# Transposing the attention weights in two halves of 64 rows, two heads at a time

## The chip, the cores and the metric

The kernel runs on one NeuronCore of a Trainium2 chip. The core has a matrix engine (TensorE, PE in the profile; its weight loads are listed apart as PEld), a vector engine (VectorE, DVE), a scalar engine (ScalarE, ACT), a general engine (GpSimd, POOL) and a synchronisation engine (SyncE, SP) that issues most DMAs. Matrix results land in PSUM, which has eight banks of 512 float32 columns on 128 partitions; everything else lives in SBUF. The metric is the device time of one execution in microseconds, lower is better.

## The reference

The program is a stack of two layers on a tensor `x` of 16 sequences of 512 tokens with 256 channels, all in float32. Four sub-layers follow each other, each with a residual and a layer norm:

1. latent attention with 16 heads: queries, keys and values are widened to 32 latent channels per head, rotated by position, and `softmax(q k^T)` is causal over 512 tokens;
2. a gated feed-forward layer whose inputs and weights are rounded to blocks of 4-bit floats;
3. a recurrence over the 512 tokens, with 16 heads of 64 states;
4. a token-mixing feed-forward layer.

The part that matters here is the attention:

```
att = einsum('bhql,bhkl->bhqk', q_for_k, k_lat) * L ** (-0.5)
att = where(causal, att, -inf); att = softmax(att, axis=-1)
y_lat = einsum('bhqk,bhkl->bhql', att, v_lat)
```

The weights `att` come out with the query token on the partitions. The second product sums over the key token, so the key token has to be on the partitions, and every 128 by 128 block of the weights is transposed in between.

## The kernel before, in words

The kernel has two long stages. The first, up to about 1757 us, does sub-layers 1 and 2, and the change is in it. The second, from about 1800 us, does sub-layers 3 and 4.

The first stage runs over 16 sequences `b`, four groups `g` of four heads, and three slots `n` (lines 799 to 834). The 512 queries are four blocks `i` of 128, and block `i` needs keys `0..i`, which is `i+1` blocks of 128 by 128. `BLOCKS` (line 521) puts block 3 in slot 0 (four key blocks), block 2 in slot 1 (three) and blocks 1 and 0 in slot 2 (two and one, three together). So each slot has four heads, and each head has three or four blocks to transpose: ten blocks per head and group, 2560 in all.

A slot goes like this.

- `scores` (line 526) issues the `S` products of its four heads into four PSUM banks. They contract over 32 latent channels, so each head uses 32 rows of the array and the four heads use different rows (line 534). VectorE then adds the mask, takes the row minimum (the scores are negated) and writes `p` to SBUF (line 546).
- `exponentials` (line 554) makes `p = exp(...)` with its row sum on ScalarE, two heads behind.
- `turn` (line 565) transposes the `p` of one head of the slot before on TensorE, three or four blocks into one PSUM bank (line 569), and ScalarE copies the bank to SBUF as `pT` (line 571).
- After the third slot of a group, `weighted` (line 576) multiplies all twelve `pT` with the values in 80 matrix instructions, four heads' worth side by side in quarters of 32 output rows (`py`, line 600).

Between these the kernel puts pieces of other work: projections (`heads` L449, `latents` L467 and L486, `values` L431, `out_projection` L501) and the feed-forward layer of an earlier sequence (`ffn_up`, `ffn_down`, which multiply through L164 and transpose at L293 and L333). `Beside.half_slot` (line 693) hands out these pieces in the order of a written plan, at an even pace, twice per head and so eight times per slot. `divide` (line 607) transposes the reciprocals of the row sums (L614) and divides `py`.

TensorE executes its instructions in exactly the order of the program text (`manual_schedule`). The other engines work through queues whose order the tile framework's planner sets when the kernel is built. Each PSUM tile of 512 columns comes from `mm` (line 152), which walks round a ring of seven banks; a tile must be read out before its bank comes round again. An eighth bank holds `py`.

The array works in shapes. Most products use all 128 rows and 128 columns. `S` uses four strips of 32 rows, the `latents` products of L467 use two halves of 64 rows (q in one, k in the other), and `py` uses four strips of 32 columns. A transpose is one matrix instruction with the data as the loaded weights and an identity as the moving operand; an ordinary float32 product takes two matrix instructions.

The pools that the change touches are `ptp`, with 14 buffers of 512 columns for `pT` (line 791), and the ring of banks.

Of the kernel before, what the change touches and what calls it, by code (L numbers as in the profile page):

```python
# [10 lines left out]
F32 = mybir.dt.float32  # L11
# [8 lines left out]
P = 128  # L20
B, T, C = 16, 512, 256
NT = T // P
# [37 lines left out]
def tile_kernel(ctx: ExitStack, tc: tile.TileContext, I: dict, out: bass.AP):  # L60
    nc = tc.nc
# [90 lines left out]
    def mm(name):  # L152
        banks.append(banks.pop(0))
        return banks[-1].tile([P, 512], F32, tag="mm", name=name)
# [198 lines left out]
    with ExitStack() as a:  # L353
# [44 lines left out]
        for i in range(2):  # L398
            nc.gpsimd.tensor_copy(bd["bdqs"][:, i::2], bd["bdq"][:, 1 - i :: 2])
            at = COLS["q2lb"][0]  # L400
# [161 lines left out]
                )  # L562
            return p

        def turn(n, p):
            w = sum(i + 1 for i, _ in BLOCKS[n]) * P
            ps = mm("ps_pt")
            for at in range(0, w, P):
                nc.tensor.transpose(ps[:, at : at + P], p[:, at : at + P], ident)  # L569
            pT = ptp.tile([P, T], F32, tag="pT", name="pT")  # L570
            nc.scalar.copy(pT[:, :w], ps[:, :w])  # L571
            return pT

        undivided = []

        def weighted(b, g, pTs):

            if g % 2 == 0:
                weighted.py = ps_y.tile([P, 2, 2, P], F32, tag="y", name="py")
            py = weighted.py[:, g % 2]  # L580

            rc = small.tile([P, 16], F32, tag="rc", name="rc")
            nc.vector.reciprocal(rc, sum_of.pop((b, g)).rearrange("p c e h -> p (c e h)"))  # L583
            rcx = att.tile([P, 2, P], F32, tag="rcx", name="rcx")
            nc.gpsimd.tensor_copy(  # L585
                rcx.rearrange("p c (n d) -> p (c n) d", d=16),
                rc.unsqueeze(2).to_broadcast([P, 16, 16]),
            )
            quarters = [[], [], [], []]
            for n, blocks in enumerate(BLOCKS):  # L590
                for i, at in blocks:
                    for h in range(4):
                        for j in range(i + 1):
                            pt = pTs[n * 4 + h][:, at + j * P : at + j * P + P]
                            quarters[PLACE[i][0] * 2 + h // 2].append((i, j, h, pt))
            for q in quarters:
                q.sort(key=lambda e: e[:3])
            for four in zip(*quarters):
                for q, (i, j, h, pt) in enumerate(four):
                    nc.tensor.matmul(  # L600
                        py[q * 32 : q * 32 + 32, PLACE[i][1], :], vpad[b % 2][:, j, g * 4 + h, :], pt,
                        start=j == 0 and h % 2 == 0, stop=j == i and h % 2 == 1,
                        skip_group_check=True,
                    )
            undivided.append((b, g, py, rcx))
# [182 lines left out]
                pass  # L788

        pp = a.enter_context(tc.tile_pool(name="pp", bufs=9))  # L790
        ptp = a.enter_context(tc.tile_pool(name="ptp", bufs=14))
        ps_b = five.enter_context(tc.tile_pool(name="ps_b", bufs=5, space=PSUM))
        ps_y = five.enter_context(tc.tile_pool(name="ps_y", bufs=1, space=PSUM))
        banks[:] = [ps_2] * 2 + [ps_b] * 5
# [3 lines left out]
        with tc.manual_schedule(engines={mybir.EngineType.PE}):  # L798
# [4 lines left out]
            for slot in slots + [None]:  # L803
# [14 lines left out]

                for h in range(4):
                    beside.half_slot()  # L820
                    if before:
                        pTs.append(turn(before[0][2], before[1][h]))
                    if slot:
                        behind.append((*slot, h, *tiles[h]))
                        ps.append(tiles[h][0])
                    while len(behind) > (LAG if slot else 0):
                        exponentials(*behind.pop(0))
                    if h == 1:
                        divide()
                    beside.half_slot()  # L830
# [484 lines left out]
```

## Time and profile before

| what | value |
|---|---|
| device time, median of 3 | 2539.11 us (2538.06 to 2540.24) |
| profiled execution, span from first to last instruction | 2543.7 us |
| mean granted TensorE clock | 0.980 |
| PE busy / DVE busy / ACT busy / POOL busy | 95% / 76% / 64% / 41% |
| transposes of `p` (L569) | 2560 matrix instructions, mean 280 ns, 396.3 us busy |
| copies to `pT` (L571) | 768, mean 517 ns, 374.2 us busy |
| products with the values (L600) | 5120 matrix instructions, mean 274 ns |

The profile gives each instruction's start and duration. Matrix instructions are pipelined: the duration of one is its way through the array, and several overlap, so the pace of a sequence is read from the starts of successive rows of the timeline and not from the mean duration. The profiled execution's span is 4.6 us above the median of the timed runs. "Idle before" in a row is the time for which the engine had nothing in flight, with the instruction that ended it.

### The profile page before, as it was taken

The page shows a single profiled execution, that of the slowest core. Times are in us where ns is not written, and L with a number is a line of the kernel's source. Part 1 is how long each engine was busy: PE and PEld are TensorE (multiplying, and loading weights), DVE is VectorE, ACT ScalarE, POOL GpSimd, SP SyncE. Part 2 cuts the span into 40 slices and gives each one's busy share as a digit, 9 for nine tenths or more (in the row PEclk, how much of TensorE's full clock was granted, in tenths as well). Part 3 has the DMA queues.
Part 4 walks back from the last instruction along what each step waited for, and adds up shares of the span by engine and source line. Part 5 has one row for each costly group of instructions (what it writes and reads, how often), then busy time and mean ns, then how long its engine had stood idle before and what let it go on. Part 6 is the DMA issues. An engine that isn't in the chain of part 4 may idle for free.

```text
span 2543.7 us, 73791 instructions
## 1 busy us (share of the span) xinstructions
PE 2412.0 (95%) x28802; PEld 1712.7 (67%) x28802; DVE 1925.8 (76%) x5492; ACT 1621.3 (64%) x5536; POOL 1035.4 (41%) x1642
## 2 busy tenths in 40 slices
PE   7789999999999999999999999998799999999998
PEld 4455666666666666666666666655678888888885
DVE  4867888788888888888888888867756666666666
ACT  4656676676766666666666666654366666666664
POOL 4322333333333333333333333332445555555554
PEclk8889999999999999999999999989899999999999
DMA  3000000000000000000000000000111111111100
GB/s 117 24 9 6 12 24 14 16 16 12 24 14 16 16 12 24 14 16 16 12 24 14 16 14 6 16 14 9 43 32 39 37 40 41 40 38 39 36 28 27
DMA packets 58015, 61.30 MB, mean 24 GB/s; under 512 B 7873, under 2 KB 53058, under 8 KB 57666
## 3 DMA queue, kind: packets, MB, share of 16 engines
q1 hardware_dynamic: 56802, 55.54, 7.0%
q8 instruction: 226, 3.70, 0.6%
q14 instruction: 123, 1.01, 0.1%
q10 hardware_dynamic: 864, 1.05, 0.1%
HBM read 39.79 MB, written 16.78 MB: 22 GB/s over the span
## 4 chain that ended last, share of the span: by engine, by line
PE 51%; DVE 29%; ACT 10%; POOL 5%; issue 3%; DMA 1%; ACTq 0%; DVEq 0%; POOLq 0%; SPq 0%
PE u L1076 8%; DVE p L546 5%; PE ps_pt L569 5%; PE u L1036 5%; ACT p L559 4%; PE S L534 3%; PE ps_d L164 3%; DVE q_q L210 3%; ACT pT L571 3%; PE pg L164 3%; PE pu L164 2%; PE ps_h L449 2%; DVE q_sc L205 2%; DVE q_q L218 2%; PE ps_a L916 2%
## 5 line engine op out<-in xcount | busy, mean ns | idle before, releaser
L559 ACT ACTIVATE p<-p,nm 128x512 f32<-128x512 f32 (+3 forms) x1024 | 570.4, 562 | 492.3 <-DVE nm L546 488.3
L1084 ACT ACTIVATE hist<-u 64x64 f32<-64x64 f32 x2048 | 447.1, 218 | 237.4 <-PE u L1076 151.4
L546 DVE CUSTOM_DVE_ANT_0 p<-S,mask 128x512 f32<-128x512 f32 (+3 forms) x1024 | 442.9, 484 | 50.9 <-PE S L534 50.4
L1076 PEld LDWEIGHTS u<-hist,ta 128*64 128x64 f32 x8176 | 367.7, 138 | 119.9 <-ACT hist L1084 41.5
L569 PEld LDWEIGHTS ps_pt<-ident,p 128*128 128x128 f32 x2560 | 302.0, 142 | 217.3 <-issue 107.1
L571 ACT COPY pT<-ps_pt 128x384 f32<-128x384 f32 (+1 forms) x768 | 374.2, 517 | 62.3 <-PE ps_pt L569 62.1
L569 PE MATMUL ps_pt<-ident,p 128*128 128x128 f32 x2560 | 396.3, 280 | 4.5 <-DVE nm L546 3.0
L1076 PE MATMUL u<-hist,ta 128*64 128x32 f32 x8176 | 394.4, 218 | 4.6 <-ACT hist L1084 4.5
L219 POOL TENSOR_TENSOR q_q<-q_q,q_m 128x704 f32<-128x704 f32 (+1 forms) x140 | 164.1, 1172 | 372.2 <-DVE q_q L218 361.5
L534 PE MATMUL S<-kc,qr 32*128 32x512 f32 (+3 forms) x2048 | 224.1, 475 | 10.5 <-ACT qr L488 7.9
L1036 PE MATMUL u<-xt,wb 128*64 128x64 f32 x4128 | 224.9, 231 | 5.1 <-issue 5.0
L559 ACT ACTIVATION_READ_ACCUMULATOR p<-p,nm 128x1 f32 x1024 | 199.8, 195 | 0.0
L164 PE MATMUL ps_d<-wdT,hT 128*128 128x256 f32 x732 | 173.1, 386 | 13.9 <-DVE nm L546 12.1
L164 PE MATMUL pg<-wgT,xqT 128*128 128x352 f32 x512 | 177.9, 471 | 6.5 <-DVE nm L546 5.1
L483 POOL TENSOR_TENSOR qc<-qc,qs 128x512 f32<-128x512 f32 x64 | 81.5, 1273 | 235.5 <-DVE qs L482 221.1
L164 PE MATMUL pu<-wuT,xqT 128*128 128x352 f32 x512 | 173.7, 462 | 1.0 <-DVE nm L546 1.0
L1036 PEld LDWEIGHTS u<-xt,wb 128*64 128x64 f32 x4128 | 166.7, 140 | 10.3 <-issue 5.5
L600 PEld LDWEIGHTS py<-pT,vpad 128*32 128x32 f32 x5120 | 138.7, 110 | 47.0 <-issue 30.3
L600 PE MATMUL py<-pT,vpad 128*32 128x128 f32 x5120 | 162.6, 274 | 7.8 <-ACT pT L571 7.5
L164 PEld LDWEIGHTS ps_d<-wdT,hT 128*128 128x128 f32 x732 | 135.4, 192 | 37.6 <-DVE nm L546 15.4
L86 POOL TENSOR_SCALAR ve<-mv 128x2 f32<-128x2 f32 (+1 forms) x160 | 31.1, 194 | 312.4 <-DVE mv L94 309.7
L585 POOL COPY rcx<-rc 128x256 f32<-128x256 f32 x64 | 40.3, 630 | 286.9 <-DVE rc L583 260.9
(167 smaller groups left out, 4648.8 us busy)
## 6 DMA issues: line engine op xcount, KB each, us to landing
xT<-in_xT_dram SPq DMA_DIRECT2D x16, 512.0 KB
x<-in_x_dram SPq DMA_DIRECT2D x16, 512.0 KB
xs<-x SPq DMA_DIRECT2D x64, 128.0 KB
x<-xs SPq DMA_DIRECT2D x32, 256.0 KB
xm<-xs SPq DMA_DIRECT2D x32, 256.0 KB
out_dram<-o SPq DMA_DIRECT2D x64, 128.0 KB
w<-in_w_down_dram SPq DMA_DIRECT2D x2, 352.0 KB
w<-in_w_gate_dram SPq DMA_DIRECT2D x5, 128.0 KB
```

Source lines behind the costliest of these rows:

```text
L164: nc.tensor.matmul(dst, left, right, start=start, stop=stop)
L219: last.tensor_tensor(q, q, m, ALU.subtract)
L483: nc.gpsimd.tensor_tensor(of[k], of[k], x, ALU.add)
L534: nc.tensor.matmul(S[h][:, at : at + w], q[rs, i * P : i * P + P], k[rs, :w], start=True, stop=True,)
L546: nc.vector.tensor_tensor_reduce(out=p[:, own], in0=S[h][:, own], in1=mask[:, T - (i + 1) * P :], scale=1.0, scalar=-MASKED, op0=ALU.add, ...
L559: nc.scalar.activation(p[:, own], p[:, own], AF.Exp, bias=nm[:, u : u + 1], scale=-1.0, accum_out=sum_of[b, g][:, cb, half, h : h + 1],)
L569: nc.tensor.transpose(ps[:, at : at + P], p[:, at : at + P], ident)
L571: nc.scalar.copy(pT[:, :w], ps[:, :w])
L600: nc.tensor.matmul(py[q * 32 : q * 32 + 32, PLACE[i][1], :], vpad[b % 2][:, j, g * 4 + h, :], pt, start=j == 0 and h % 2 == 0, stop=j == i ...
L1036: nc.tensor.matmul(u[rs, k, par:n:2, bs : bs + 16], wb[:, g * 2 + k, par, half, rs], xt[:, g, at : at + n - par : 2, :], start=par == 0 an ...
L1076: nc.tensor.matmul(into[cs, :, c, :], ta[:, t % 2, g * 2 + k, cs], own[:, :, c, :], start=False, stop=True, skip_group_check=True,)
L1084: nc.scalar.activation(state[g][rs, :, r * 32 : r * 32 + 32].rearrange("p k (s b) -> p k s b", s=2), u[rs, :, t - t0, :] .rearrange("p k ( ...
```

## The change

`turn` now takes two heads. It asks for two PSUM banks. Every block of `p` is cut into its upper and lower 64 rows (64 query tokens each), and each half is transposed by an instruction of its own with a 64 by 64 piece of the identity: the upper half through rows 0 to 63 of the array into the first bank, the lower half through rows 64 to 127 into the second. A bank thus holds the same half of all blocks of both heads, with 64 columns per block. Two copies on ScalarE, one per bank, put the halves side by side in a `pT` tile of 2 x 512 columns, so that a block is again 128 contiguous columns for `weighted`. The loop calls `turn` at the second and fourth head of a slot for two heads at once. `ptp` has 7 buffers of twice the size.

```diff
-        def turn(n, p):
-            w = sum(i + 1 for i, _ in BLOCKS[n]) * P
-            ps = mm("ps_pt")
-            for at in range(0, w, P):
-                nc.tensor.transpose(ps[:, at : at + P], p[:, at : at + P], ident)
-            pT = ptp.tile([P, T], F32, tag="pT", name="pT")
-            nc.scalar.copy(pT[:, :w], ps[:, :w])
-            return pT
+        def turn(n, two):
+
+            w = sum(i + 1 for i, _ in BLOCKS[n])
+            ps = [mm("ps_pt") for _ in range(2)]
+            halves = [t.rearrange("p (u n t) -> p u n t", u=2, t=64) for t in ps]
+            for u, p in enumerate(two):
+                for at in range(w):
+                    for r in range(2):
+                        rs = slice(r * 64, r * 64 + 64)
+                        nc.tensor.transpose(
+                            halves[r][:, u, at, :], p[rs, at * P : at * P + P], ident[rs, rs],
+                        )
+            pT = ptp.tile([P, 2, NT, 2, 64], F32, tag="pT", name="pT")
+            for r in range(2):
+                nc.scalar.copy(pT[:, :, :w, r, :], halves[r][:, :, :w, :])
+            return pT.rearrange("p u n r t -> p u (n r t)")
...
-                            pt = pTs[n * 4 + h][:, at + j * P : at + j * P + P]
+                            pt = pTs[n * 2 + h // 2][:, h % 2, at + j * P : at + j * P + P]
...
-        ptp = a.enter_context(tc.tile_pool(name="ptp", bufs=14))
+        ptp = a.enter_context(tc.tile_pool(name="ptp", bufs=7))
...
-                    if before:
-                        pTs.append(turn(before[0][2], before[1][h]))
+                    if before and h % 2:
+                        pTs.append(turn(before[0][2], before[1][h - 1 : h + 1]))
```

## The prediction

> **What bounds the kernel now.** I read the page's slices first, then the busy time of the steady stretch, then the chain that ended last over the attention stage, then the groups of the changed lines by shape, and last the PE timeline for the pace of single instructions.
>
> ```profile
> PE   7789999999999999999999999998799999999998
> ...
> 370.00:1525.00 1155.00, 1121.83 (x9183) 762.07 (x9181) 958.13 (x2807) 775.23 (x2313) 414.11 (x480) 1.00 0.05 16
> ```
>
> The second line has PE, PEld, DVE, ACT and POOL busy in 1155 us of the steady stretch: PE 97%, DVE 83%, ACT 67%, at full granted clock. The change lies only in the stage up to 1757 us.
>
> ```profile
> by line: DVE p L546 7.5%; PE ps_pt L569 7.4%; ACT p L559 5.8%; PE S L534 4.9%; PE ps_d L164 4.6%; DVE q_q L210 4.5%; issue 3.8%; ACT pT L571 3.8%; PE pg L164 3.6%; PE pu L164 3.5%; DVE q_q L218 3.4%; DVE q_sc L205 3.4%; PE ps_h L449 3.3%; D
> ```
>
> This is the chain over 45 to 1757 us. PE is almost always occupied, yet the chain runs through VectorE about as often: in each sequence of some 106 us there are stretches of 30 us in which PE work follows PE work, and stretches of 20 and 40 us in which VectorE does and PE is barely ahead. The transposes have 7.4% of 1712 us, 127 us.
>
> ```profile
> L569 PE MATMUL ps_pt<-ident,p 128*128 128x128 f32 x2560 | 396.3, 280 | 4.5 <-DVE nm L546 3.0 <-ACT xqT L295 0.7 <-ACT pT L571 0.4
> ...
> L571 ACT COPY pT<-ps_pt 128x384 f32<-128x384 f32 x512 | 228.9, 482 | 38.8 <-PE ps_pt L569 38.6
> ...
> L571 ACT COPY pT<-ps_pt 128x512 f32<-128x512 f32 x256 | 145.4, 587 | 23.5 <-PE ps_pt L569 23.5
> ```
>
> The pace, and what a change of the array's shape costs, is in the timeline (start, length of the row, engine, line, count):
>
> ```profile
> 104.52 0.20 PEld L235 LDWEIGHTS ps_t<-ident,wq 64*128 64x128 f32 x2 [0.56 <-POOL wq L220]
> 104.53 0.33 PE L235 MATMUL ps_t<-ident,wq 64*128 64x64 f32 x2 [0.32 <-DVE nm L546]
> ...
> 916.66 0.49 PE L569 MATMUL ps_pt<-ident,p 128*128 128x128 f32 x3
> 916.99 1.89 PE L431 MATMUL ps_v<-wv,xT 128*128 128x256 f32 x8
> ...
> 920.28 0.55 PE L569 MATMUL ps_pt<-ident,p 128*128 128x128 f32 x3
> 920.75 0.69 PE L467 MATMUL ps_qs<-heads,bdqs 64*128 64x512 f32 x1
> ...
> 925.64 0.69 PE L467 MATMUL ps_q<-heads,bdq 64*128 64x512 f32 x1
> 925.65 0.69 PE L467 MATMUL ps_k<-heads,bdk 64*128 64x512 f32 x1
> 926.17 0.59 PE L467 MATMUL ps_q<-heads,bdq 64*128 64x512 f32 x1
> 926.18 0.59 PE L467 MATMUL ps_k<-heads,bdk 64*128 64x512 f32 x1
> 926.70 0.66 PE L569 MATMUL ps_pt<-ident,p 128*128 128x128 f32 x4
> ...
> 1398.54 0.49 PE L569 MATMUL ps_pt<-ident,p 128*128 128x128 f32 x3
> 1398.96 0.62 PE L600 MATMUL py<-pT,vpad 128*32 128x128 f32 x10
> 1400.07 2.17 PE L600 MATMUL py<-pT,vpad 128*32 128x128 f32 x70 [0.49 <-ACT pT L571]
> ```
>
> Three transposes followed by work of the same shape take 916.99 - 916.66 = 0.33 us, so 109 ns each. Three between works of other shapes take 920.75 - 920.28 = 0.47 us: 0.14 more, which is the first weight load no longer hidden (row of 0.55 us instead of 0.49, some 55 ns) and about 90 ns to empty the array. Leaving the 64-row shape also takes 90 ns (926.70 - 926.18 = 0.52 us for 512 columns, which take 0.43 us elsewhere), and a plain product then shows its load too (0.69 instead of 0.59 us, 104 ns). The q and k products in the two row halves start 0.01 us apart and both run at full pace.
>
> **The change part by part.**
>
> *Transposes.* Out go 2560 x 109 ns = 279 us of PE pace. In come 5120 half transposes, two per block. The trace has four 64-row transposes, all in one half of the array (L235): the second load starts 0.20 - 0.138 = 0.06 us after the first, and the second matrix instruction (223 ns long, the shortest of that tile) starts 0.33 - 0.223 = 0.11 us after the first, of which 55 ns are the unhidden load. So one half costs 57 ns, with its load hidden beside the one before. If the two halves run beside each other, as the q and k products do, a block costs 57 ns: 2560 x 57 = 146 us. If they don't, it costs 2 x 57 = 114 ns: 292 us. I take 57, since the q and k rows are the nearest case of two row halves with float32 operands and separate banks, and keep 114 for the range. Issuing is no limit: the 70 `py` instructions of the last line above start within 2.17 - 0.27 = 1.9 us, with as many loads, 14 ns per instruction; two halves with their loads are four instructions in 57 ns, the same pace.
>
> A rule of the skill speaks against this. The row says that a 64-row load of 128 columns lets the next one start after 0.06 us. The Trainium skill ("TensorE: Matmul & The Clock Gate", section on LDWEIGHTS) says that a weight load takes its columns divided by 1.2 in nanoseconds, however few rows it has; that would be an estimated 107 ns per half, the load would set the pace, and the sum below would turn from a saving into an estimated 30 us of loss. The trace's plain loads agree with the page (104 ns), its transposes' loads don't (55 ns), and the measured row decides.
>
> *Changes of shape.* I went through PE's instructions between the first and the last transpose of `p` in trace order, and counted places where the shape (128 x 128, 64 or 32 rows, or 32 columns) differs from the instruction before: 626. With each even head's transposes moved to behind those of the odd head, and all of them of 64-row shape, it is 1040. Going in costs 93 ns + 55 ns for the load, coming out 90 ns + 104 ns (55 where another transpose follows): 171 ns on average. 414 x 171 ns = 71 us more. The gain from next to the L467 products, which have the same shape, is in this count.
>
> *PE in sum:* -133 + 71 = -62 us of 1712.
>
> *What of that reaches the end.* 127 of the transposes' 279 us lie on the chain, a share of 0.45. The rest lies where VectorE's queue sets the pace and PE would only wait longer. -62 x 0.45 = -28 us. The ends: nothing of it passes, or all of it (-62).
>
> *Copies.* 768 before and after, of the same 384 or 512 elements per partition; the reads are two runs per bank, the writes runs of 64. A copy of 256 elements in runs of 16 (`vpad`, L437) has a mean of 371 ns and a contiguous one (`rT`, L616) 376, so I count no change in length. They lie beside PE work on an engine that is 67% busy. What changes is when they come: two in a row after every second head. Behind them in ScalarE's queue wait exponentials, the tanh of the gate (L309) and the copies of others; VectorE waits on that tanh for 94 us in all.
>
> *The wait before `py`.* In the third group of each sequence `py` follows the last transposes directly, and already waits 0.49 us for the last copy (1400.07). Now both copies of the last pair must be done before the first product with either head: one more copy, 0.48 us, 16 times, 8 us. In the other three groups 1.1 to 2.4 us of other PE work lie in between, which cover 0.97 us of copies and the way to them, the 1.1 us just so. The 8 us count at the same 0.45: +4 us. Queued behind `py` are the next slot's `S`, on which VectorE's line 546 waits.
>
> *Earlier demands that fall away.* Heads 0 and 2 are transposed about two half slots later, so their exponentials are surely ready; these waits were 3.0 us (row of L569) and I count nothing. Bank use is unchanged in number, two at a time out of the ring of seven, and `pT` has the same bytes.
>
> *Sum:* -28 + 4 = -24 us on the profiled execution's 2543.7, so 2519.7; that execution lies 4.6 us above the median of the runs, so 2515 us.
>
> **The rivals.**
>
> 1. *The halves don't run beside each other.* For it: no row shows two transposes in two row halves. Against it: q and k. Price: 292 - 279 + 71 = +84 us of PE; at 0.45 +38, and as PE then binds nearly everywhere up to all of it: 2577 to 2623 us. The point from which it decides is 81 ns per block: (279 - 71)/2560.
> 2. *VectorE takes over.* It is 83% busy with 17 us of idle time in 106, most of it waits of about 1 us for POOL and ScalarE. If its queue absorbs what PE gains, the time is 2534 to 2544. For it speaks the chain's VectorE share, against it the PE stretches of 30 us per sequence.
> 3. *ScalarE's paired copies delay VectorE.* If each of the 128 tanh of the gate waits one copy (0.48 us) longer and VectorE with it, that is +61 us, or -28 + 61 = +33 at worst; half of it gives 2541, and the range is 2544 to 2572. For it: the chain already goes exponentials, two copies, tanh, VectorE. Against: before, these copies also stood there, only one at a time.
> 4. *All of PE's gain passes*, since PE is 97% busy: 2543.7 - 62 - 4.6 = 2477, to 2495.
>
> **How the numbers follow.** My forecast, a share of about one half passing, 2495 to 2534: 0.49. Rival 1: 0.17. Rival 2: 0.11. Rival 3: 0.12. Rival 4: 0.11. A range of 2480 to 2570 leaves out rival 1 and a little of rivals 3 and 4, 2 in 10; the likeliest case alone is 2495 to 2534. A difference of 0.2% (5 us) is about what a measurement of this kernel can tell from none: faster 0.60, same 0.11, slower 0.29.
>
> **What would show it.** Right: 5120 transposes of shape 64*128 with 64x64 operands, pairs starting about 57 ns apart with the second half a few ns behind the first; stretches of 0.34 us (six pairs) or 0.46 us (eight) plus about 0.34 us of changing; PE's share falls and its waits for VectorE grow; copies still 482 and 587 ns. Wrong: halves that start 57 ns apart in turn, so 114 per block (rival 1); `py` waiting 1 us and more in more than one group; more idle time of VectorE before line 310 (rival 3); a chain with PE's share unchanged and longer transposes. The forecast falls if a change of shape costs more in the new place than between L569 and L467, or if the planner orders VectorE's queue in another way.

## The result, and the profile after

The change makes the kernel slower: 2556.66 us (median of 4, 2553.82 to 2559.43) beside 2539.68 us (2538.06 to 2543.98) for the kernel before. The ratio is 1.0063, with a 95% interval of 1.0049 to 1.0078. The prediction was 2515 us. The time lies inside the range given with it (2480 to 2570), but on the other side of the time before, so the direction was wrong.

The profiled execution of the kernel after has a span of 2557.6 us, 13.9 more than that of before. First the slices of its page: busy tenths of TensorE and VectorE, and the granted clock.

```profile
PE   7778999999999999999999999997799999999998
...
DVE  6756788887878878888787887887756666666666
...
PEclk9789999999999999999999999999899999999999
```

TensorE's start is emptier than before (7, 7, 7, 8 in the first slices, 7, 7, 8, 9 before), and the rest of its row reads almost the same. The steady stretch, with the same columns as before (PE, PEld, DVE, ACT, POOL, clock, DMA):

```profile
370.00:1525.00 1155.00, 1106.04 (x10823) 708.17 (x10822) 943.18 (x2772) 761.20 (x2274) 404.04 (x473) 1.00 0.05 16
```

TensorE is busy for 15.8 us less of the 1155 than before (1121.83), and VectorE and ScalarE also do less in the same time (958.13 and 775.23 before): all three wait more. The chain of work that ended last, over the attention stage (45 to 1771 us):

```profile
by line: DVE p L546 12.0%; PE S L534 5.9%; ACT p L559 5.6%; PE py L608 5.4%; DVE q_q L210 4.6%; issue 4.3%; PE ps_pt L574 4.0%; PE ps_h L449 3.9%; PE pg L164 3.9%; ACT pT L579 3.8%; PE pu L164 3.3%; DVE q_sc L205 3.1%; DVE q_m L214 2.7%; DV
```

The transposes fell from 7.4% to 4.0% of it, as they should. In their place VectorE's line 546, which reads the `S` banks, went from 7.5% to 12.0%, and `py` is in it with 5.4%. The groups of the changed lines (L574 are the half transposes, L579 the copies; busy us in all, mean ns of one, idle time before them):

```profile
L574 PE MATMUL ps_pt<-ident,p 64*128 64x64 f32 x5120 | 251.1, 231 | 12.3 <-DVE nm L546 8.9 <-ACT pT L579 2.1 <-DVE qc L477 0.6
...
L579 ACT COPY pT<-ps_pt 128x384 f32<-128x384 f32 x512 | 218.0, 483 | 58.3 <-PE ps_pt L574 58.1
...
L579 ACT COPY pT<-ps_pt 128x512 f32<-128x512 f32 x256 | 137.1, 593 | 9.9 <-PE ps_pt L574 9.1
```

Four rows of TensorE's timeline in the kernel after (start, length of the row, line, count):

```profile
1250.46 0.59 PE L574 MATMUL ps_pt<-ident,p 64*128 64x64 f32 x12
1250.97 1.14 PE L534 MATMUL S<-kc,qr 32*128 32x512 f32 x8
...
1371.93 0.66 PE L574 MATMUL ps_pt<-ident,p 64*128 64x64 f32 x16
1372.52 0.44 PE L622 MATMUL ps_r<-ident,rcx 128*128 128x128 f32 x2
```

These rows carry the change's own mechanism. Eight pairs that follow work of the same shape take 1372.52 - 1371.93 = 0.59 us with the way out of the shape; six that come after another shape take 1250.97 - 1250.46 = 0.51 us. Starts inside a turn show a new pair every 61 to 64 ns (mean 62.7; the second pair after a change of shape comes 111 ns behind the first, as the load shows) and the second half mostly 3 to 4 ns behind the first. So the halves do run beside each other. The copies keep their 483 and 593 ns (482 and 587 before).

What TensorE waits for in the steady stretch of the kernel before (line that waits, what released it, us in total, times, longest):

```profile
PE ps_d L164 <- DVE nm L546: 10.4, 11, 1.0
...
PE py L600 <- ACT pT L571: 4.3, 11, 0.5
...
PE ps_xq L293 <- ACT rT L616: 2.5, 2, 1.3
...
PE ps_pt L569 <- DVE nm L546: 0.4, 1, 0.4
```

and of the kernel after:

```profile
PE ps_v L431 <- DVE nm L546: 12.2, 11, 1.1
PE ps_d L164 <- ACT hT L335: 9.4, 11, 0.9
PE py L608 <- ACT pT L579: 7.0, 10, 0.7
PE ps_xq L293 <- ACT rT L624: 3.5, 2, 1.8
...
PE ps_pt L574 <- DVE nm L546: 2.9, 10, 0.4
```

The row of `ps_v` takes the place of the one in which `ps_d` waited for the same line 546; behind it stands a PSUM bank that VectorE has not yet read. `ps_d` now waits for `hT` instead, and `py`, `ps_xq` and the transposes wait longer than before. TensorE is idle for 45.8 us in these 1155, against 31.5 in the kernel before. VectorE's waits in the same stretch of the kernel before:

```profile
DVE th L310 <- ACT th L309: 63.2, 54, 2.7
DVE x L100 <- POOL rstd L88: 34.2, 43, 1.2
...
DVE yT L621 <- ACT rT L616: 14.9, 22, 0.9
```

and of the kernel after:

```profile
DVE th L310 <- ACT th L309: 73.7, 55, 3.6
DVE x L100 <- POOL rstd L88: 42.7, 42, 1.5
...
DVE yT L629 <- ACT rT L624: 24.1, 33, 1.5
```

VectorE waits longer for the tanh, for GpSimd's part of the norm and for the reciprocals' copy, 28 us in these three rows. So the saved time of TensorE did not vanish in one place. The waits grew on both sides of the hand-offs.

To see where the 13.9 us lie I cut both spans at the starts of the sequences (the first `S` product of each); time at half clock is counted from 30 us on:

| part of the span | before | after | time at half clock, before and after |
|---|---|---|---|
| up to the start of sequence 3 | 354.4 | 365.9 | 45.6 and 72.0 |
| sequences 3 to 14 | 1277.2 | 1290.2 | 0 and 10.2 |
| sequence 15, to the last `py` | 128.3 | 118.8 | 13.7 and 0 |
| rest | 783.7 | 782.8 | |

Sequence 15 is the one part in which the kernel after is clearly ahead, by 9.5 us. The 13.7 us at half clock there belong to the kernel before; their cause is open.

In sequence 11, an undisturbed one, I also estimated TensorE's need: the time its instructions would take at full clock if each started as soon as the pace of its kind allows, from the start-to-start distances of the same traces. It fell from 99.2 to 96.0 us, and the rest of the period rose from 6.8 to 10.3: the period went from 106.0 to 106.3.

### The profile page after: what moved, and what is told of

Its sections match the earlier page's. It is cut to its first block, busy times and chain, and to the rows that moved or that the text cites. A ratio compares the mean times of both kernels' runs of the same rounds, so it can differ in the third digit from the quotient of the medians.

```text
span 2557.6 us, 78855 instructions
## 1 busy us (share of the span) xinstructions
PE 2396.3 (94%) x31362; PEld 1644.1 (64%) x31362; DVE 1927.1 (75%) x5492; ACT 1618.5 (63%) x5536; POOL 1031.5 (40%) x1642
## 4 chain that ended last, share of the span: by engine, by line
PE 50%; DVE 30%; ACT 9%; POOL 5%; issue 4%; DMA 1%; SPq 1%; ACTq 0%; DVEq 0%; POOLq 0%
DVE p L546 8%; PE u L1084 8%; PE u L1044 5%; PE S L534 4%; ACT p L559 4%; PE py L608 4%; DVE q_q L210 3%; PE ps_pt L574 3%; PE pg L164 3%; PE ps_h L449 3%; ACT pT L579 3%; DVE q_sc L205 2%; PE pu L164 2%; PE ps_a L924 2%; PE ps_k L924 2%
## 5 line engine op out<-in xcount | busy, mean ns | idle before, releaser
L579 ACT COPY pT<-ps_pt 128x384 f32<-128x384 f32 (+1 forms) x768 | 355.1, 519 | 68.1 <-PE ps_pt L574 67.2
L574 PEld LDWEIGHTS ps_pt<-ident,p 64*128 64x128 f32 x5120 | 200.8, 140 | 183.1 <-issue 76.3
L574 PE MATMUL ps_pt<-ident,p 64*128 64x64 f32 x5120 | 251.1, 231 | 12.3 <-DVE nm L546 8.9
L534 PE MATMUL S<-kc,qr 32*128 32x128 f32 (+3 forms) x2048 | 243.7, 479 | 13.6 <-DVE nm L546 7.5
L164 PE MATMUL pg<-wgT,xqT 128*128 128x352 f32 x512 | 186.2, 486 | 2.1 <-ACT xqT L295 1.2
L608 PE MATMUL py<-pT,vpad 128*32 128x128 f32 x5120 | 169.5, 278 | 17.1 <-ACT pT L579 16.8
L1044 PEld LDWEIGHTS u<-xt,wb 128*64 128x64 f32 x4128 | 166.8, 140 | 10.3 <-issue 5.6
L534 PEld LDWEIGHTS S<-kc,qr 32*128 32x128 f32 x2048 | 113.0, 187 | 75.5 <-issue 18.6
```

The costliest lines, as they stand in the source:

```text
L164: nc.tensor.matmul(dst, left, right, start=start, stop=stop)
L534: nc.tensor.matmul(S[h][:, at : at + w], q[rs, i * P : i * P + P], k[rs, :w], start=True, stop=True,)
L574: nc.tensor.transpose(halves[r][:, u, at, :], p[rs, at * P : at * P + P], ident[rs, rs],)
L579: nc.scalar.copy(pT[:, :, :w, r, :], halves[r][:, :, :w, :])
L608: nc.tensor.matmul(py[q * 32 : q * 32 + 32, PLACE[i][1], :], vpad[b % 2][:, j, g * 4 + h, :], pt, start=j == 0 and h % 2 == 0, stop=j == i ...
L1044: nc.tensor.matmul(u[rs, k, par:n:2, bs : bs + 16], wb[:, g * 2 + k, par, half, rs], xt[:, g, at : at + n - par : 2, :], start=par == 0 an ...
```

## The experiments

The question is why a TensorE that needs 51 us less (16 sequences of 3.2, by that estimate) ends 17 us later. The change has three parts that can be taken apart: pairing the heads, halving the blocks, and the copies that come in pairs. The theories at the start were that VectorE's total work takes over as the pace (theory A in the expectations), that the late copies delay others (theory B), and that changes of shape and waiting for a whole pair cost more on TensorE's part of the chain than the halves save (theory C). Each time is the median of 4 to 10 executions. The ratio is to the kernel before on the same chip, which took 2539 to 2543 us, so differences between rows of different chips are good to some 4 us.

| kernel | us | ratio, 95% interval |
|---|---|---|
| pairs_whole | 2530.34 | 0.9957 (0.9943 to 0.9971) |
| fewer_blocks | 2525.29 | 0.9932 (0.9917 to 0.9947) |
| pairs_early | 2592.64 | 1.0202 (1.0186 to 1.0217) |
| after_padded | 2588.81 | 1.0183 (1.0167 to 1.0198) |
| before_less_dve | 2534.39 | 0.9970 (0.9958 to 0.9981) |
| after_less_dve | 2554.16 | 1.0047 (1.0031 to 1.0064) |
| pairs_less_dve | 2528.43 | 0.9945 (0.9929 to 0.9960) |
| pairs_switch | 2590.65 | 1.0187 (1.0172 to 1.0203) |
| pairs_pool_m | 2692.83 | 1.0596 (1.0572 to 1.0620) |
| pairs_interleaved | 2532.60 | 0.9969 (0.9956 to 0.9982) |
| after_first | 2540.51 | 1.0004 (0.9994 to 1.0013) |
| pairs_first | 2538.70 | 0.9994 (0.9984 to 1.0003) |
| after_copies_first | 2557.69 | 1.0059 (1.0044 to 1.0074) |
| pairs_copies_first | 2531.55 | 0.9958 (0.9943 to 0.9973) |
| after_no_sums | 2538.89 | 0.9989 (0.9978 to 0.9999) |
| pairs_no_sums | 2530.60 | 0.9960 (0.9946 to 0.9973) |
| after_filled | 2572.66 | 1.0125 (1.0110 to 1.0140) |
| after_whole_start | 2543.83 | 1.0013 (1.0002 to 1.0025) |

### One part alone: pairs of whole blocks

The kernel before with the turns of two heads at the second and fourth head, but whole transposes, a bank and a copy for each head (the lines of `turn` that are new):

```diff
+        def turn(n, two):
+            w = sum(i + 1 for i, _ in BLOCKS[n])
+            ps = [mm("ps_pt") for _ in range(2)]
+            for u, p in enumerate(two):
+                for at in range(w):
+                    nc.tensor.transpose(
+                        ps[u][:, at * P : at * P + P], p[:, at * P : at * P + P], ident
+                    )
+            pT = ptp.tile([P, 2, T], F32, tag="pT", name="pT")
+            for u in range(2):
+                nc.scalar.copy(pT[:, u, : w * P], ps[u][:, : w * P])
...
```

> The pairing alone: two heads at a time at the second and fourth head, into two banks, but whole transposes of 128 rows, one bank and one copy per head. TensorE's need is as before, without the added changes of shape. Theory A (VectorE's queue sets the pace, what TensorE saves turns into waits, and waits drop its clock): 2535 to 2550 us. Theory B (coming late and in twos costs what the halves save): the pairing alone loses what was lost, 17 us, and what the halves should have won, some 28 us, so 2570 to 2595 us.

It is 12 us faster than the kernel before and 26 us faster than the kernel after, below both bands. So pairing by itself is a gain here, the loss comes with the halves (by themselves, or by what the planner makes of them, which is taken up below), and this version beats both kernels. In the profiled executions it is 17.3 us ahead of the kernel before, and 10.5 of these lie in sequence 15 (117.8 us against 128.3), 1.8 in sequences 3 to 14. Its steady stretch, same columns:

```profile
370.00:1525.00 1155.00, 1126.38 (x9194) 770.67 (x9194) 957.32 (x2814) 770.81 (x2312) 411.91 (x481) 1.00 0.05 16
```

TensorE is busier than in either kernel, at the same granted clock.

### Pairs one head earlier

```diff
-                    if before and h % 2:
-                        pTs.append(turn(before[0][2], before[1][h - 1 : h + 1]))
+                    if before and h % 2 == 0:
+                        pTs.append(turn(before[0][2], before[1][h : h + 2]))
```

> The changed kernel with the pairs turned at the first and third head of a slot instead of the second and fourth, so that the last copies have two half slots more before the products with the values. Theory A: as the changed kernel, 2545 to 2565 us. Theory B: 10 to 30 us below the changed kernel, 2525 to 2545 us.

36 us slower than the kernel after, with the same instructions, and outside both bands; a steady sequence takes 109.6 us instead of 107.4 (medians of sequences 4 to 14). TensorE's waits in the steady stretch show a part of it: the transposes, which waited 2.9 us for VectorE's line 546 in the kernel after, now do so for

```profile
PE ps_pt L574 <- DVE nm L546: 14.4, 10, 1.5
```

Moved one head ahead, a turn meets a bank that line 546 has not emptied. That is 11.5 us more of waiting in 1155; sequences 3 to 14 are 28 us longer. Where a turn stands matters more here (36 us) than the whole change did (17).

### What TensorE time is worth: less of it, and more of it

1024 of the 2560 whole transposes of the kernel before are left out, and the copies read the transposed columns twice, so `pT` holds wrong blocks:

```diff
-            for at in range(0, w, P):
+            for at in range(0, 2 * P, P):
...
-            nc.scalar.copy(pT[:, :w], ps[:, :w])
+            some = ps[:, : w // 2].unsqueeze(1).to_broadcast([P, 2, w // 2])
+            nc.scalar.copy(pT[:, :w].rearrange("p (r n) -> p r n", r=2), some)
```

> The kernel before with two transposes per head instead of four or three: 1024 of the 2560 are left out, and the copies, unchanged in number and size, read the transposed columns twice. No pairs, no halves, no added changes of shape; TensorE needs 1024 x 109 ns = 112 us less. Theory A: little or nothing of it reaches the end, 2525 to 2560 us, with more time at half clock. The share of 0.45 from the prediction: -50 us, 2490 us.

112 us of TensorE out (1024 x 109 ns), 17 us gained: 0.15 of it, and not the 2490 us that the share of 0.45 gives. This is the most direct reading of what a saving is worth. TensorE's need in sequence 11 fell from 99.2 to 92.4 us and its waits rose from 6.8 to 12.5. The steady stretch, same columns as before, has TensorE busy for 27.6 us less than in the kernel before:

```profile
370.00:1525.00 1155.00, 1094.27 (x8589) 706.28 (x8588) 964.39 (x2820) 772.71 (x2316) 405.99 (x483) 1.00 0.05 16
```

The other direction, in the kernel after: the first block of each head is transposed twice, 47 us of TensorE more.

```diff
-                for at in range(w):
+                for at in [*range(w), 0]:
```

> The changed kernel with the first block of each head transposed twice: two more pairs of half transposes per turn, 384 x 2 x 61 ns = 47 us more of TensorE's time. Theory A: the added work fills waits and keeps the clock up, 2535 to 2560 us, not slower than the changed kernel. If TensorE sets the pace for 0.45 of the stage: +21 us, 2578 us.

It costs 32 us, 0.68 of what was added, more than either case of the expectation. Changes of shape by themselves, on the pairs of whole blocks: one pair of half transposes, overwritten at once, ahead of each turn, so two more changes of shape per turn.

```diff
+            for r in range(2):
+                rs = slice(r * 64, r * 64 + 64)
+                nc.tensor.transpose(ps[r][:, :64], two[r][rs, :P], ident[rs, rs])
```

> Pairs with whole transposes, 2530 us, plus one pair of half transposes ahead of each turn, which the whole ones overwrite: two changes of shape per turn, 93 + 55 + 61 + 90 + 55 = 354 ns, 384 times, 136 us of TensorE's time. Theory A: 7 us of waits per sequence swallow much of it, up to 40 us slower, 2530 to 2575 us. Theory C: most of it shows, as in the padded kernel (32 us for 47 us), 2610 to 2650 us.

The expectation counts 136 us of TensorE; the need worked out in sequence 11 rose by 6.7 us (99.0 to 105.7), 107 us in all. 60 us are lost, 0.44 to 0.56 of it. The time lies between the two bands. So a microsecond put on TensorE costs about half of itself and more, and one taken off is worth a sixth. The three shares come from three kernels close to each other, each with its own order of the other queues. Even a shift by 16 us, the largest that a priority alone makes below, would leave at most 0.3 for the saving and at least 0.3 for the added work. These kernels stand at the bend between the two, and a price read at the one side does not hold on the other.

### VectorE's total work

Line 215 (the scaling of `m`, on VectorE) is left out, 59 us of VectorE less; the rounding of the 4-bit blocks is then wrong.

```diff
-        nc.vector.tensor_scalar(m, m, 1.0, 1.5 * 2.0**22, ALU.max, ALU.mult)
```

> The kernel before without one VectorE instruction per quantisation (line 215, the clamp and scale of the rounding constant), left out and not replaced: 59 us less of VectorE work in the first stage, nothing else touched. Theory A (VectorE's queue sets the pace): 20 to 50 us faster, 2490 to 2520 us. Theory C (the added changes of shape and the copies that both wait for the whole pair lie on TensorE's part of the chain): little change here, 2530 to 2540 us, as TensorE is the pace before too.

> The changed kernel with the same VectorE instruction left out. Theory A: with VectorE relieved TensorE's saving shows, so it is as fast as or faster than the kernel before with the same cut, 2475 to 2515 us. Theory C: the distance to the kernel before with the same cut stays at 15 us or more.

The kernel before gains 9 us, the kernel after 2.5, and the distance between them stays 20 us, both as theory C has it (TensorE is the pace before and after). If VectorE's work set the pace after the change, the kernel after would have gained the more. Theory A falls. The same line moved to GpSimd on the pairs of whole blocks:

> Pairs with whole transposes, and the VectorE instruction of line 215 moved to GpSimd, which is 36% busy in the steady stretch: 59 us of VectorE become some 120 us of GpSimd in a chain of dependent steps. Theory A: VectorE relieved, 10 to 30 us faster than the pairs alone, 2500 to 2520 us, if the longer way over GpSimd is covered. Theory C: no faster than the pairs alone, 2530 to 2545 us.

It is 162 us slower than pairs_whole, outside both bands, and the page's chain by line has the moved line in the second place:

```profile
PE u L1081 7%; POOL q_m L215 7%; DVE p L546 6%; PE S L534 4%; PE u L1041 4%; PE ps_pt L571 4%; ACT p L559 3%; PE py L605 3%; PE pg L164 3%; DVE q_q L210 3%; PE pu L164 3%; PE ps_d L164 2%; PE ps_h L449 2%; DVE q_sc L205 2%; PE ps_a L921 2%
```

VectorE's next line needs this result. GpSimd is the idlest of the four engines in the kernels before and after (41% and 40% busy), but a line that is moved there between two lines of VectorE adds two hand-offs, whatever VectorE is spared. So this run says nothing on theory A.

### Late copies

In the kernel after, neither bank is complete before the last block of both heads, so both copies come at the end. The same on whole blocks: the blocks of the two heads alternate.

```diff
-            for u, p in enumerate(two):
-                for at in range(w):
+            for at in range(w):
+                for u, p in enumerate(two):
```

> Pairs with whole transposes (2530 us), but the blocks of the two heads take turns, so that neither bank is complete before the end of the pair, as in the changed kernel; the first copy can start 0.3 to 0.4 us later. TensorE's need is the same. Theory C (copies that wait for the whole pair cost what the halves save): 2538 to 2555 us. If that order does not matter: 2527 to 2535 us.

2532.60 us, 2 us behind pairs_whole and in the band for an order that does not matter. Late copies are not the cause.

### The order of the other queues

TensorE's order is written out, but the planner orders the other queues, and it plans anew for each program. In a steady sequence the order of VectorE's instructions in the kernels before and after agrees to 0.94 (share of matching sequence, in sequence 11), ScalarE's to 0.87. To set another order, line 546, which empties the `S` banks, was given priority in the kernel after and in the pairs of whole blocks:

```diff
-                    nc.vector.tensor_tensor_reduce(
+                    with tc.high_priority():
+                        nc.vector.tensor_tensor_reduce(
...
```

> The changed kernel with line 546 (mask, minimum and p from S, which frees the S banks) put first in the planner's order of VectorE. Theory D (what TensorE saves goes into waiting for banks that hold S until VectorE comes to read them): 10 to 40 us faster than the changed kernel, 2515 to 2545 us. If the banks are not what it waits for: 2550 to 2560 us, or slower where the other VectorE work now comes too late.

> The same priority for line 546 in the kernel with pairs of whole transposes. Theory D: 5 to 30 us faster than the pairs alone, 2500 to 2525 us, less than in the changed kernel, as TensorE waits less here. Otherwise 2528 to 2540 us.

With this order the kernel after is 16 us faster than without, the pairs of whole blocks 8 us slower, and they differ by 2 us. The first is what theory D has, the second is not. The same for the two copies of a pair:

> The kernel after, with a higher priority for the two copies of each pair in the planner's order of ScalarE. To be read against its twin with whole transposes. If the halves themselves are worth about nothing and the 26 us between the kernel after and the paired whole transposes come with the order that the planner happens to give the other engines' queues, another order moves this distance: the two differ by less than 10 us, either way, as they did by 2 us with the priority on line 546. If the halves cost time by themselves, the distance stays at 20 us or more.

> Paired whole transposes, with the same higher priority for the copies: the twin of the run before this one. Order theory: within 10 us of it. Halves cost by themselves: this one is 20 us or more ahead. If late copies held anything up, both would gain; the alternating blocks showed about 2 us, so no gain over 2530 us is expected here.

The distance is 26 us again. But the trace shows that this priority changed next to nothing: in sequence 11 the order of VectorE's instructions is the same as without it in both kernels, and ScalarE's almost, and so the pair repeats the first one rather than testing another order. A third pair without the row sums of the exponentials (set to one), which takes work from ScalarE:

```diff
-                    accum_out=sum_of[b, g][:, cb, half, h : h + 1],
```

> The kernel after without the row sums of the exponentials (they are set to one, so the softmax is not divided by its sum): the exponentials' instructions on ScalarE stay and the accumulator reads behind them go, some 200 us of ScalarE's time on the way from S over the exponentials to the transposes. If the way through the hand-offs S, minimum, exponential, transposes, copy sets the period of a sequence, this is 30 to 100 us faster than the kernel after. If ScalarE has no part in it, it is less than 10 us faster.

> Paired whole transposes without the row sums in the same way. If the way through ScalarE sets the period, 30 to 100 us faster than the paired whole transposes; and then TensorE binds sooner, so that its twin with halves, which needs 3 us less of TensorE per sequence, gains more than this one and comes out up to 20 us ahead of it. If ScalarE has no part, less than 10 us faster and the distance of 26 us between the twins stays.

The kernel after gains 18 us, less than the 30 expected of a way through ScalarE that sets the period, and the pairs of whole blocks gain nothing. Neither theory of that expectation holds as written: ScalarE is not what holds the period at 106 us, since ScalarE's busy time per sequence fell from 70.8 to 65.7 us and the median period only from 107.4 to 106.6 and from 106.3 to 106.1. What did change is the distance, to 8 us. And the last pair, without VectorE's line 215:

> Paired whole transposes without VectorE's line 215 (the scaling of m, 59 us of VectorE in the whole run, left out: the scales of the 4-bit blocks are wrong). Its twin with halves took 2554.2 us. If the distance between halves and whole blocks belongs to the halves, this kernel is at 2524 to 2532 us, 22 to 30 us ahead of its twin. If the distance belongs to the order that the planner happens to give, it can take any value, as it took 2 us and 8 us in two other twins; 2535 us or more would speak for that.

26 us ahead of its twin after_less_dve, inside the band of a distance that belongs to the halves. Five pairs, then: 26 (nothing else changed), 26 (priority for the copies), 26 (without line 215), 2 (priority for line 546) and 8 us (without the row sums). In none of them are the halves ahead, although TensorE needs 3 us less per sequence with them.

Cut at the starts of the sequences, the profiled executions of these pairs have the halves behind by 14, 7, 6, 2 and 2 us up to the start of sequence 3, and by 15, 15, 16, -4 and 3 us in sequences 3 to 14. In the mean of all executions the halves have 43, 45, 34, 35 and 11 us more at half clock. So more time at half clock goes with the halves in every pair, and what they cost in the steady part depends on what else is changed.

### The start, and the clock

The time up to the start of sequence 3 is 365.9 us in the kernel after and 351.9 in pairs_whole, with 72.0 and 25.0 us of it at half clock. To fill the waits, half transposes in the first two sequences were done three times, 616 pairs or some 38 us of TensorE more:

```diff
-                for at in range(w):
+                for at in [*range(w)] * times:
...
+                        pTs.append(turn(before[0][2], before[1][h - 1 : h + 1], 3 if b < 2 else 1))
```

> The changed kernel with every half transpose done three times in the turns of the first two sequences: 24 turns x 2 x about 0.7 us = 35 us more of TensorE's time before about 260 us, where the changed kernel had 72 us at half clock. Theory E (the clock falls in TensorE's waits and costs about half of the time spent at half clock): fewer than 45 us at half clock there, and 2545 to 2565 us. If the clock plays no part: 35 us x 0.7 as in the padded kernel, 2575 to 2585 us.

The time at half clock in the start fell to 40.7 us, and the run still lost 16 us, in neither band. Added work and regained clock can't be told apart here, so by itself this run is inconclusive. The last run doesn't add anything: whole blocks in sequences 0 to 2, halves from 3 on.

```diff
+            if whole_blocks:
+                for u, p in enumerate(two):
+                    for at in range(w):
+                        nc.tensor.transpose(
+                            ps[u][:, at * P : at * P + P], p[:, at * P : at * P + P], ident
+                        )
...
+                        pTs.append(turn(before[0][2], before[1][h - 1 : h + 1], before[0][0] < 3))
```

> The kernel after, with whole transposes (same pairs) in sequences 0 to 2 and halves from sequence 3 on. The kernel after stands 26 us behind the paired whole transposes: 14 us of it up to the start of sequence 3, where it has 72 us at half clock against 25, and 15 us in sequences 3 to 14. If the halves themselves cost the 14 us of the start, this kernel is at 2539 to 2546 us, with 25 to 45 us at half clock in the start. If the start is slow for another reason, it stays at 2552 to 2560 us.

2543.83 us: 13 us of the 26 come back, inside the band. The start takes 351.7 us, as in pairs_whole, with 28.2 us at half clock. The order of VectorE's instructions in sequence 11 is the one of the kernel after, and the steady median stays at 107.4 us. So about half of the loss is made in the first three sequences when they have halves. The 14 us are not a fixed price of the halves: in the other four pairs they are 2 to 7 behind at this point, the other traces with whole blocks in pairs (without pairs_switch and pairs_pool_m) get there between 351.7 and 359.5 us, and the profiled execution of pairs_whole is at the early end of these. Two windows of the start of the kernel after (same columns as above, the granted clock is the third number from the right):

```profile
30.50:133.60 103.10, 86.06 (x794) 49.61 (x794) 69.71 (x224) 68.20 (x212) 34.11 (x39) 0.81 0.12 35
...
166.00:208.00 42.00, 32.87 (x252) 19.31 (x250) 25.32 (x71) 19.48 (x56) 11.69 (x13) 0.80 0.00 1
```

and the same windows of after_whole_start:

```profile
30.50:133.60 103.10, 87.06 (x667) 52.91 (x668) 72.16 (x233) 72.10 (x224) 34.38 (x40) 0.92 0.12 35
...
166.00:208.00 42.00, 35.69 (x297) 23.66 (x300) 29.84 (x76) 22.37 (x64) 9.95 (x9) 0.91 0.01 1
```

The longest wait there is one of `S` for a bank that VectorE reads, in the timeline of the kernel after:

```profile
172.23 2.07 PE L534 MATMUL S<-kc,qr 32*128 32x512 f32 x2 [5.05 <-DVE nm L546]
```

and in that of after_whole_start:

```profile
164.57 2.07 PE L534 MATMUL S<-kc,qr 32*128 32x512 f32 x2 [4.14 <-DVE nm L546]
```

In the start little other work stands beside the attention, and TensorE waits for VectorE and ScalarE. In the 42 us from 166 it is busy 32.87 us with halves and 35.69 with whole blocks, and the clock is 0.80 and 0.91 (the second kernel is some 8 us further on in its work there, 172.23 - 164.57 in these rows).

What a microsecond at half clock is worth can be read from the executions themselves, since every one has its own mean clock. Within each of the 20 programs of this study I set the span of each execution against its time at half clock (twice the lacking share of the clock times the span). Over some 170 executions the span rises by 0.31 us for each us at half clock, and this explains 62% of the spread between executions of one program. The kernel after has 119 us at half clock over the whole span and pairs_whole 76, in the mean of their runs: 43 x 0.31 = 13 us, as much as the start lost; for the other pairs it is 14, 11, 11 and 4 us. That is an agreement between two readings and not a proof: no run held the clock up and left all else alone. It also fits after_filled: 31 us less at half clock are worth 10, the 38 us added cost 26 at after_padded's 0.68, and 26 - 10 = 16 stand beside 16 measured.

### What is left in the steady part

After_whole_start still needs 10.6 us more than pairs_whole in sequences 3 to 14 (1286.0 and 1275.4 us). The kernel after needs 14.8 more. Half of its sequences there take 106.3 to 106.7 us, 0.5 to 1.0 more than the same ones of pairs_whole; sequences 5, 12 and 13 take 109.3 to 109.7, which is 2.4 to 2.7 more each. The second group of sequence 12 is the second of these two windows of the kernel after; the first is the same group of sequence 11:

```profile
1251.00:1276.90 25.90, 24.57 (x256) 15.95 (x254) 19.67 (x61) 15.86 (x47) 9.58 (x12) 1.00 0.02 6
1357.20:1386.10 28.90, 26.03 (x260) 16.87 (x256) 19.86 (x62) 16.33 (x47) 9.56 (x12) 0.94 0.02 6
```

and this row of TensorE's timeline lies in it:

```profile
1374.72 0.41 PE L293 MATMUL ps_xq<-ident,xq 128*128 128x128 f32 x2 [1.76 <-ACT rT L624]
```

The wait of 1.76 us is followed by 3.4 us at half clock from 1375.2. The sum of the steady sequences is 1290.2 us in the kernel after, 1274.4 with priority for line 546 and 1276.6 without the row sums, where TensorE's need (96.0, 96.0 and 95.8 us in sequence 11) is the same. So this part of the loss is not one that the halves bring with them whatever stands beside them: the priority run changes nothing but the order of the other queues, and in that order the halves are even 4 us ahead of whole blocks here (1274.4 and 1278.6). Without line 215 the halves stay 16 us behind. Which instructions have to change places, and whether the halves themselves bring about the worse order, was not found.

## Why the prediction was wrong, by its steps

*Transposes: right.* A pair takes 62.7 ns in the mean instead of the 57 worked out from one half; 5.7 ns x 2560 = 15 us more. Rival 1 (the halves don't run beside each other) is refuted by the starts, 3 to 4 ns apart. By an estimate from the Trainium skill ("TensorE: Matmul & The Clock Gate", section on LDWEIGHTS), 128 columns divided by 1.2, there would be two loads of 107 ns per pair. The runs show one pair per 61 to 64 ns, both loads included, so the measured row was the right one to take.

*Changes of shape and TensorE in sum: right.* The forecast was -133 + 71 = -62 us, with 1040 changes of shape; the trace of after has 1039. With the 15 us above it is -47, and the need estimated from the traces fell by 3.2 us per sequence, 51 in all.

*What of that reaches the end: this step failed.* The share of 0.45 was read from the chain: 127 of the transposes' 279 us lie on it. That is a statement on where the chain runs now and not on what happens when the link becomes shorter. The kernel before stands at a bend: more TensorE work costs 0.44 to 0.68 of itself, less work gives 0.15 (17 of 112 us in fewer_blocks). The median period of a steady sequence stayed between 105.4 and 108.0 us whether TensorE needed 92, 96 or 99 us, and whether VectorE had some 4 or ScalarE 5 us less per sequence. With 0.15 the sum of the prediction would have been some -7 + 4, about no change. What is measured beyond that lies in two places for which the prediction had no term.

*The first place* is the start: in the first three sequences TensorE has little other work to fill the waits. The clock was at half speed for 47 us longer there than with whole blocks, and the start took 14 us longer; with whole blocks in these three sequences alone both went away, and 13 us came back at the end. The profile of before had shown the place, in the first slices of its page and in 45.6 us at half clock up to sequence 3, and the prediction treated all sixteen sequences alike. In the other pairs the start cost 2 to 7 us, so the size of this term is open.

*The second* is the order in which the planner puts the other queues, which the prediction named last, as what would make the forecast fall. In the steady part the kernel after is 11 to 15 us behind pairs_whole, and with the priority on line 546 it is level with it (1274.4 and 1275.4 us). That this loss can be removed by the order alone is shown by this one run; that the order is what made it is argued, and why the halves got the worse one was not found.

*Copies: right.* 483 and 593 ns, and their being late costs 2 us.

*The wait before `py`: right in kind, half the size.* TensorE's waits for `pT` at `py` rose from 4.3 to 7.0 us in 1155 us, once per sequence. That is 4 us in 16 sequences, where the prediction had 8 us of waiting and let 4 of them reach the end.

*Earlier demands that fall away: left at nothing.* The prediction counted nothing for heads 0 and 2 being transposed later, on the 3.0 us of the row of L569. These waits ended on VectorE's line 546 and not on an exponential. Pairing alone gave 12 us, most of it in sequence 15. That this is because of the later demand is not shown. In the profiled executions the parts are -17 us for the pairs, +14 for the start with halves, +15 for the steady part and +2 for the rest, together the +14 between before and after.

*Rivals 2, 3 and 4.* VectorE did take a larger part of the chain, but not by its total work (before_less_dve and after_less_dve). The time lies in rival 3's range by chance: its mechanism holds only in part, as waits for the tanh grew by 10.5 us in the steady stretch, and late copies alone cost 2. Rival 4, all of the saving, is refuted by the time.

## What to carry to other kernels

In this kernel a share of the chain of waits (0.45) was near the price of work that is added (0.44 to 0.68) and far from that of work taken away (0.15); before forecasting a gain, leave the work out on a spare kernel and see what comes back. Look at the stretches with the least work beside the change first: here the faster TensorE waited longer there, and at a lower clock (0.80 and 0.81 against 0.91 and 0.92). When a change has two parts, run each alone: the pairs without the halves were the better kernel, at 2530 us.

## What the runs showed of the hardware

- Half transposes of float32 in the two row halves, to two banks, run beside each other: one pair per 61 to 64 ns, against 109 ns for a whole block. Entering and leaving the 64-row shape takes 93 to 94 ns each: from the last `pu` product to a turn 390 ns against 296 to a whole transpose, and from the last pair to a `pg` product 155 ns against 62 to another pair.
- The time at half clock comes in pieces of 3.4 us (3.4, 6.8, 10.2, 17.1 in the kernel after), and a single wait of 1.76 us was followed by one of them in a stretch that was otherwise at full clock. Not every such wait is: of the 78 waits of TensorE over 1.5 us between 370 us and sequence 15 in the 20 traces, 26 were (13 of these in pairs_pool_m, which has 25 of the waits).
- A microsecond at half clock lengthens this kernel by 0.31 us in the spread of its executions. The Trainium skill ("TensorE: Matmul & The Clock Gate", Terms) puts the penalty at one half of the time at half rate; here, where TensorE partly waits for others, the runs give less.
- The spread between executions of one program, some 5 us here, is for more than half the clock's: 62% of it goes with the time at half clock.
- With transposes added to the start, the time at half clock there fell from 72.0 to 40.7 us. The Trainium skill (the same page, "PE-mode transpose") has it that transposes don't count as work for the clock in the same way; in after_filled the time at half clock fell with nothing but transposes added, though the order of the other queues in the start changed with them.
